# First batch's autoregressive taps as three single-pass products of two-term operands, and second terms loaded first at the joint of two attentions

## The chip, the cores and the metric

The kernel runs on one core of one Trainium2 chip. The metric is the device time of one execution in microseconds (us). A profiled execution gives the time of every instruction; its span is the time from the first to the last instruction in the profile.

## The reference, cut to what matters

An image batch of 2 x 128 channels x 64 x 64 passes through two layers. Layer 0 normalises in groups, forms queries, keys and values, adds rotary positions, attends over the 4096 positions in 4 heads, projects and adds. Layer 1 works on tokens t (2 x 4096 x 128):

```python
t = t + _L1_attn_ref(_ln_t(t))        # softmax(x x^T) x, unscaled, one head
t = t + _L1_ffn_ref(_ln_t(t), ...)    # spectral filters + autoregressive taps

def _compute_ar_u(Mu, u):             # Mu: (3, 128, 128)
    out = jnp.zeros(u.shape[:2] + (Mu.shape[-1],), dtype=u.dtype)
    for i in range(Mu.shape[0]):
        ui = jnp.pad(u, ((0, 0), (i, 0), (0, 0)))[:, :sl]
        out = out + jnp.einsum('btd,de->bte', ui, Mu[i])
    return out
```

The last step also convolves u with 16 spectral filters of full length, mixes the 16 results with 128 x 128 matrices, and does all of this on four prefixes of the sequence (whole, half, quarter, eighth), of which a softmax with a fixed Gumbel noise picks one (y_hard - y_soft + y_soft as weights). So one branch's taps `mu`, matrices and prefix length count; the kernel finds them at run time. All is float32.

## The kernel before, in words

One core does both batches in one instruction stream per engine. TensorE (PE) multiplies, VectorE (DVE), ScalarE (ACT) and GpSimd (POOL) work beside it, SyncE (SP) issues most DMAs. Waits between engines are placed by the framework. Within an engine it may also choose the order by readiness; instructions given to `keep_in_program_order` (layer 0's products L190, the layer norm's `normed` L716, the conv stage's matmuls through `ordered` L1133) stay in the order in which the code issues them. The generators passed as `beside` are advanced one step at a time between the pieces of the main work, so the code interleaves them by hand.

**Layer 0** (`layer0`, L175). For each batch, pair of heads and block of 512 positions it makes scores (L190), exponentials (L443), and weighted sums (L190 too), whose rows `close` (L386) copies to `accs` (L391). `divide` (L335) then adds the three value terms (L346, L348), takes reciprocals of the row sums by way of DRAM (L345, L349, L351, L352) and multiplies; `project` (L358) applies the output matrix. The last unit's `divide` (wait = 5) and `project` are not done when the attention ends; they go on as the generator `left` beside the next stage.

**Products of two terms.** Many operands are float32r pairs: a first term (a copy rounded to float32r) and a second term (the difference). A product is then three passes: first x first, first x second, second x first. `hiT`/`loT` hold the normalised tokens transposed, `hi`/`lo` untransposed. The second terms of batch 0 do not fit beside layer 0, so `normalise(0)` (L752) stores them in DRAM (`lows`, 8 chunks of two 128 x 512 tiles) and `ready(i)` (L1087) loads them back: for i = 0 the chunks 0 and 1, then chunk i + 1; each load goes into a tile `low` (one buffer, 512 KB), and two copies (L1092 to `loT`, L1093 to `lo`) follow.

**Attention of layer 1** (`attend`, L897), once per batch, over pairs of blocks (j, i), i from j to 7, of 512 tokens. `scores` (L906): three products a tile (L911), exponential on ACT (L920). `turn` (L924): transposes (L927), copy (L929), subtraction (L930). `sums` (L964): splits e into two terms (L968 on DVE or ACT, L969 on DVE), multiplies (`weigh`, L937), adds to `oT` (L975, L977). `close` (L945): the block's division and addition to the tokens (L948, L956, L959), then `closed(j)`.

- `attend(0)` runs beside `left`, batch 1's statistics, `filters` (L803), `matrices` (L857, with `branch_weights` L822: z at L830 and a chain of small DVE operations to wbr, coef at L872) and `normalise(1)` (L719, L766, L770). The transform table `fw` (L796) is loaded before it.
- `attend(1)` runs beside `feed(0)` (L1007): layer norm, transforms, and taps of batch 0. After each block, `closed(j)` (L1114) also loads two of the 16 mixing matrices (`m`, L1119, two buffers) and splits them.

**The taps** (`taps`, L1015; tiles of 512 tokens). `uT` holds 6 columns of 128 x 128: tokens transposed (L1051) and masked (L1052), and before them the last two columns of the tile before (L1054). Three float32 products per tile, of one matrix of `mu` each and four neighbouring columns of `uT` (L1024), are summed in PSUM, added to the tokens (L1027) and stored (`base`). Tile 0 needs the end of tile 7, so its taps come last (L1069 to L1077).

**The conv stage** (`convolve` L1176, `mix` L1203, `back` L1232) follows for both batches, its PE order written out; `feed(1)` runs beside it, with the same code for the taps.

Of the kernel before, what the change touches and what calls it, by code (L numbers as in the profile page):

```python
# [22 lines left out]
P = 128  # L23
# [12 lines left out]
NU = 3  # L36
# [27 lines left out]
def conv_attn_hybrid(ctx: ExitStack, tc: tile.TileContext, io):  # L64
# [110 lines left out]
    def layer0(tok, px, last, side, beside_last):  # L175
# [3 lines left out]
        with ExitStack() as l0:  # L179
# [155 lines left out]
            def divide(b, h, c, accs, wait):  # L335

                u = f"{b}_{h}_{c}"
                if h == 0:  # L340
                    ao[b, c] = (last if c == 3 else p1).tile([P, 1024], F32, tag=f"ao{c}", name=f"ao{b}_{c}", bufs=1)
                own = ao[b, c][CH * h : CH * h + CH, :]
                parts = [accs[CH * n : CH * n + CH, :] for n in range(NV)]
                rec = last.tile([CH, 1024 // CH], F32, tag="rec", name=f"rec{u}")
                nc.sync.dma_start(rec, accs[NV * CH :, :].rearrange("o (r s) -> o r s", r=CH))  # L345
                nc.vector.tensor_tensor(own, parts[0], parts[1], ALU.add)  # L346
                yield
                nc.vector.tensor_tensor(own, own, parts[2], ALU.add)  # L348
                nc.vector.reciprocal(rec, rec)  # L349
                back = dram.tile([CH, 1024 // CH], F32, tag="rec", name=f"back{u}", bufs=4)  # L350
                nc.sync.dma_start(back, rec)  # L351
                nc.sync.dma_start(parts[0], back.rearrange("r s -> (r s)").partition_broadcast(CH))  # L352
                for _ in range(wait):
                    yield
                nc.vector.tensor_tensor(own, own, parts[0], ALU.mult)
                yield
# [377 lines left out]
    def layers(st, layer0):  # L734
# [87 lines left out]
        def branch_weights(p):  # L822
# [4 lines left out]
            nc.gpsimd.dma_start(lg[:, 0, :], io["log_weights"].partition_broadcast(P))  # L827
            nc.gpsimd.dma_start(lg[:, 1, :], io["gumbel"].partition_broadcast(P))
            z = p.tile([P, NBR], F32, name="z")
            nc.vector.tensor_tensor(z, lg[:, 0, :], lg[:, 1, :], ALU.add)  # L830
            zm = p.tile([P, 1], F32, name="zm")
            nc.vector.tensor_reduce(zm, z, AX.X, ALU.max, negate=True)
            zs = p.tile([P, 1], F32, name="zs")
# [170 lines left out]
            for _ in beside:  # L1004
                pass

        def feed(b, p, bank, fw, stats=None):  # L1007


            if stats is None:  # L1010
                stats = LayerStats(p, tok[b], f"f{b}")
                yield from stats.steps()
            to = rows[b].rearrange("c r w d -> w c r d")

            def taps(i, uT):  # L1015
                oc = p.tile([P, 4, P], F32, tag="oc", name=f"oc{b}_{i}", bufs=1)
                pt = bank(f"tT{b}_{i}").rearrange("p (t c) -> p t c", c=C)
                for t in range(4):
                    nc.tensor.transpose(pt[:, t, :], tok[b][:, 4 * i + t, :], ident)
                nc.scalar.copy(oc, pt)  # L1020
                yield
                pa = bank(f"ar{b}_{i}").rearrange("p (t c) -> p t c", c=C)
                for n in range(NU):
                    nc.tensor.matmul(pa, mu[:, n, :], uT[:, 2 - n : 6 - n, :], start=(n == 0), stop=(n == NU - 1))  # L1024
                    if n == 0:
                        yield
                nc.vector.tensor_tensor(oc, pa, oc, ALU.add)  # L1027
                nc.sync.dma_start(base[b][:, 4 * i : 4 * i + 4, :], oc)
                yield

            before = first = None
            for i in range(NQ):
# [12 lines left out]
                    nc.sync.dma_start(to[:, c, at : at + 2, :], uhr[:, :, 1, :])  # L1045
                    yield

                uT = p.tile([P, 6, P], F32, tag="uT0" if i == 0 else "uT", name=f"uT{b}_{i}", bufs=1 if i == 0 else 2)
                pt = bank(f"uT{b}_{i}").rearrange("p (t c) -> p t c", c=C)
                for t in range(4):  # L1050
                    nc.tensor.transpose(pt[:, t, :], un[:, t, :], ident)  # L1051
                nc.vector.tensor_tensor(uT[:, 2:, :], pt, mask.unsqueeze(1).to_broadcast([P, 4, P]), ALU.mult)  # L1052
                if i:
                    nc.vector.tensor_copy(uT[:, :2, :], before[:, 4:, :])  # L1054
                    yield
                    yield from taps(i, uT)
                else:
# [4 lines left out]
            for c in range(2):  # L1062
# [3 lines left out]
            nc.sync.dma_start(to[:, :, BP, :], ul)  # L1066
            yield

            nc.gpsimd.memset(first[:, :2, 0:1], 0.0)  # L1069
            nc.vector.tensor_tensor(  # L1070
                first[:, :2, 1:],
                before[:, 4:, : P - 1],
                mask[:, 1:].unsqueeze(1).to_broadcast([P, 2, P - 1]),
                ALU.mult,
            )
            yield
            yield from taps(0, first)  # L1077

        with ExitStack() as l1:
            p1 = pool(l1, "l1")  # L1080
            lo.append(p1.tile([P, L], F32R, name="lo"))
            fw = transform(p1)
            with ExitStack() as part:
                p = pool(part, "l1_a")
                gate = [0]

                def ready(i):  # L1087
                    for n in range(2) if i == 0 else [i + 1]:
                        if n < NQ:
                            low = p.tile([P, 2, 512], F32, tag="low", name=f"low{n}")  # L1090
                            nc.sync.dma_start(low, lows[n].rearrange("n p c -> p n c"))
                            nc.vector.tensor_copy(loT[0][:, bass.ts(n, 512)], low[:, 0])  # L1092
                            nc.vector.tensor_copy(lo[0][:, bass.ts(n, 512)], low[:, 1])  # L1093

                def closed(j):
                    gate[0] = j + 1
# [13 lines left out]
            with ExitStack() as part:  # L1110
# [3 lines left out]
                def closed(j):  # L1114
                    fed.take(range(4 * j, 4 * j + 4))
                    fed.close(range(4 * j, 4 * j + 4))
                    own = slice(2 * j, 2 * j + 2)
                    m = p.tile([P, 2, 2, C], F32, tag="m", name=f"m{j}")
                    nc.sync.dma_start(m, mx[own].rearrange("k p s c -> p k s c"))  # L1119
                    nc.vector.tensor_copy(mxr[:, own], m)  # L1120
                    nc.vector.tensor_tensor(mxl[:, own], m, mxr[:, own], ALU.subtract)

                attend(1, p1, feed(0, p, bank, fw), closed)
        psum_a.close()


# [325 lines left out]
```

## Time and profile before

| what | value |
|---|---|
| median of 3 runs | 2924.3 us (2923.44 to 2927.81) |
| profiled execution | 2924.81 us |
| its span | 2923.0 us |
| mean granted clock of TensorE | 0.993 of full speed |
| chain that ended last | the conv stage: m L1218, bk L1272, vt L1262 on PE |
| layer 0's exponentials, L443 on ACT | 937.4 us in 704 instructions |
| layer 0's scores and sums, L190 on PE | 557.7 and 557.1 us |
| conv stage's mixing, L1218 on PE (three groups) | 409.5, 403.0, 291.8 us |
| loads tables_in<-tables on SP | 1024 of 64 KB, 3.3 us from issue to landing |

The profiled execution's time is 1.8 us more than its span. A group of the profile names the line, engine, operation, the tile written and the tiles read, then count, busy time and mean length; a matmul's length includes its latency, so neighbouring matmuls overlap, and the spacing of their starts tells what one costs. A float32 matmul leaves two records. The waits of an engine name the line that waited, the engine and line that released it, and the time. The layer-0 attention ends and the first attention of layer 1 begins near 1028 us; the second attention begins near 1396 us and ends before 1770 us.

### The profile page before, as it was taken

The page shows a single profiled execution, that of the slowest core. Times are in us where ns is not written, and L with a number is a line of the kernel's source. Part 1 is how long each engine was busy: PE and PEld are TensorE (multiplying, and loading weights), DVE is VectorE, ACT ScalarE, POOL GpSimd, SP SyncE. Part 2 cuts the span into 40 slices and gives each one's busy share as a digit, 9 for nine tenths or more (in the row PEclk, how much of TensorE's full clock was granted, in tenths as well). Part 3 has the DMA queues.
Part 4 walks back from the last instruction along what each step waited for, and adds up shares of the span by engine and source line. Part 5 has one row for each costly group of instructions (what it writes and reads, how often), then busy time and mean ns, then how long its engine had stood idle before and what let it go on. Part 6 is the DMA issues. An engine that isn't in the chain of part 4 may idle for free. (4 is left out here: it accounts for less than half of the span.)

```text
span 2923.0 us, 40062 instructions
## 1 busy us (share of the span) xinstructions
PE 2852.4 (98%) x13872; PEld 1815.1 (62%) x13872; DVE 1689.9 (58%) x2916; ACT 1916.1 (66%) x2507; POOL 653.8 (22%) x1312
## 2 busy tenths in 40 slices
PE   5999999999999999999999999999999999999998
PEld 3555555555455577787777885666666666666665
DVE  5265562355243289877866677555555555555554
ACT  4999999999999956565555664444444444444442
POOL 3022120022000010000102003343444444444440
PEclk9999999999999999999999999999999999999999
DMA  4122120021001024100011002333333334333331
GB/s 137 33 63 77 48 66 16 5 78 48 6 33 35 4 83 128 57 1 1 26 39 40 8 26 68 97 89 93 92 85 82 81 77 115 82 85 84 82 82 54
DMA packets 166033, 175.91 MB, mean 60 GB/s; under 512 B 45264, under 2 KB 109536, under 8 KB 165824
## 3 DMA queue, kind: packets, MB, share of 16 engines
q1 hardware_dynamic: 122528, 137.05, 16.9%
q0 software_dynamic: 40304, 32.99, 5.4%
q10 hardware_dynamic: 2992, 3.22, 0.3%
q8 instruction: 115, 1.88, 0.3%
q14 instruction: 94, 0.77, 0.1%
HBM read 130.68 MB, written 25.49 MB: 53 GB/s over the span
## 5 line engine op out<-in xcount | busy, mean ns | idle before, releaser
L443 ACT ACTIVATE e<-s 128x1536 f16<-128x1536 f32 (+1 forms) x704 | 937.4, 1427 | 34.8 <-PE s L190 29.6
L1196 DVE TENSOR_TENSOR xl<-cv,xh 128x1024 fp32r<-128x1024 f32 x512 | 603.2, 1220 | 436.3 <-ACT xh L1195 349.0
L1195 ACT CAST xh<-cv 128x1024 fp32r<-128x1024 f32 x512 | 494.6, 1018 | 522.7 <-PE cv L1186 511.8
L1161 POOL DMA_DIRECT2D tokens_in<-rows x1024 | 490.5, 487 | 680.0 <-PE cv L1186 580.7
L190 PE MATMUL s<-qs,ks 128*128 128x512 f16 x2048 | 557.7, 379 | 11.8 <-ACT e L443 7.4
L190 PE MATMUL acc<-e,v 128*97 128x512 f16 x2048 | 557.1, 379 | 3.3 <-DVE accs L391 0.2
L1218 PE MATMUL m<-xh,loT 128*128 128x512 f32 x1024 | 409.5, 400 | 0.0
L1218 PE MATMUL m<-xh,hiT 128*128 128x512 f32 x1024 | 403.0, 394 | 0.0
L190 PEld LDWEIGHTS <-v 128*97 128x97 bf16 x2048 | 254.5, 124 | 214.3 <-issue 11.8
L190 PEld LDWEIGHTS <-ks 128*128 128x128 f16 x2048 | 200.5, 99 | 232.6 <-issue 46.9
L920 ACT ACTIVATE ey<-y,nshift 128x512 f32<-128x512 f32 x288 | 195.9, 689 | 201.4 <-PE y L911 179.2
L1186 PE MATMUL cv<-tables_in,tokens_in 32*128 32x512 f32 x2048 | 300.3, 646 | 1.8 <-DVE xl L1196 1.8
L1218 PE MATMUL m<-xl,hiT 128*128 128x512 f32 x1024 | 291.8, 417 | 1.2 <-DVE xl L1196 0.5
L1218 PEld LDWEIGHTS m<-xl,hiT 128*128 128x128 f32 x1024 | 178.6, 189 | 175.7 <-issue 104.7
L1218 PEld LDWEIGHTS m<-xh,loT 128*128 128x128 f32 x1024 | 192.5, 188 | 90.7 <-issue 47.8
L1218 PEld LDWEIGHTS m<-xh,hiT 128*128 128x128 f32 x1024 | 192.3, 188 | 42.2
L930 DVE TENSOR_TENSOR eT<-eT,eT 128x512 fp32r<-128x512 f32 x224 | 147.3, 684 | 112.9 <-ACT eT L929 112.0
L937 PE MATMUL oacc<-ep,hi 128*128 128x512 f32 x576 | 209.1, 411 | 1.2 <-DVE ep L969 1.2
L969 DVE TENSOR_TENSOR ep<-ey,ep 128x512 fp32r<-128x512 f32 x288 | 191.3, 684 | 7.6 <-PE oacc L937 1.4
L391 DVE COPY accs<-acc 97x512 f32<-97x512 f32 x64 | 44.2, 691 | 253.3 <-PE acc L190 253.3
L929 ACT ACTIVATE eT<-eT 128x512 fp32r<-128x512 f32 x224 | 133.1, 605 | 55.7 <-PE eT L927 55.5
L937 PE MATMUL oacc<-eT,hi 128*128 128x512 f32 x448 | 154.1, 405 | 2.2 <-DVE oT L975 1.2
(197 smaller groups left out, 3031.3 us busy)
## 6 DMA issues: line engine op xcount, KB each, us to landing
tables_in<-tables SPq DMA_DIRECT2D x1024, 64.0 KB, 3.3
tab<-in_rot SPq DMA_DIRECT2D x32, 512.0 KB, 4.1
tokens_in<-rows POOLq DMA_DIRECT2D x1024, 16.0 KB, 3.2
rows<-uh SPq DMA_DIRECT2D x64, 128.0 KB, 1.9
qs<-term POOLq DMA_DIRECT2D x112, 64.0 KB, 2.0
ks<-term POOLq DMA_DIRECT2D x96, 64.0 KB, 1.9
accs<-back SPq DMA_DIRECT2D x32, 128.0 KB, 2.3
lows<-stage SPq DMA_DIRECT2D x16, 256.0 KB, 2.0
```

The costliest lines, as they stand in the source:

```text
L190: tc.keep_in_program_order(nc.tensor.matmul(*args, **kw))
L443: nc.scalar.activation(e[:, own, :], ps[:, own, :], AF.Exp, scale=SCORE_SCALE)
L920: nc.scalar.activation(e[:, 2 * h + q, :], ps[:, q, :], AF.Exp, bias=nshift, accum_out=den[:, t, i : i + 1])
L929: nc.scalar.activation(eT[0], pt, AF.Copy, accum_out=den[:, 4 * i + u, j : j + 1])
L930: nc.vector.tensor_tensor(eT[1], pt, eT[0], ALU.subtract)
L937: nc.tensor.matmul(acc, a[0][:, own], c, start=(start and t == 0 and n == 0), stop=(stop and t == len(es) - 1 and n == 2),)
L969: nc.vector.tensor_tensor(es[t][1], e[:, t, :], es[t][0], ALU.subtract)
L1161: nc.gpsimd.dma_start(ut[part, :, :], rows[b][ci, row : row + BP, w0 : w0 + WC // 2, :])
L1186: nc.tensor.matmul(pu[:, h, :], ut[grp, w % 2, :], tt[grp, w % 2, :], start=True, stop=True)
L1195: nc.scalar.copy(hi, pu.rearrange("d h (c k) -> d k h c", k=NK))
L1196: nc.vector.tensor_tensor(seconds[n % 2][:, :, w, 64 * g2 : 64 * g2 + 64].rearrange("d k (h c) -> d k h c", h=2), pu.rearrange("d h (c k) ...
L1218: nc.tensor.matmul(acc, m, x, start=(s == 0 and w == 0 and i == 0), stop=(s == 1 and w == WC - 1 and i == len(products) - 1),)
```

## The change

`feed` takes a new argument `parts`, set for the first batch alone. With it, `mu` and the masked `uT` are each split into two float32r terms by a copy and a subtraction (`split`), the columns that are taken over from the tile before are copied for both terms, and each tap is three products instead of one float32 product; the masked columns go through a tile that shares the buffer of `oc`, and tiles 1 to 7 share one buffer a term for `uT`. `ready(i)` becomes `second_parts`: chunk 0 is issued ahead of the load of `fw`, and `ready(i)` issues chunk i + 1 alone. Its first copy, the sum z in `branch_weights`, and the first sum of the last `divide` are kept in program order. The tile `m` has one buffer instead of two.

```diff
@@ -343,7 +343,9 @@
                 parts = [accs[CH * n : CH * n + CH, :] for n in range(NV)]
                 rec = last.tile([CH, 1024 // CH], F32, tag="rec", name=f"rec{u}")
                 nc.sync.dma_start(rec, accs[NV * CH :, :].rearrange("o (r s) -> o r s", r=CH))
-                nc.vector.tensor_tensor(own, parts[0], parts[1], ALU.add)
+                terms = nc.vector.tensor_tensor(own, parts[0], parts[1], ALU.add)
+                if wait > 1:
+                    tc.keep_in_program_order(terms)
                 yield
                 nc.vector.tensor_tensor(own, own, parts[2], ALU.add)
                 nc.vector.reciprocal(rec, rec)
@@ -827,7 +829,7 @@
             nc.gpsimd.dma_start(lg[:, 0, :], io["log_weights"].partition_broadcast(P))
             nc.gpsimd.dma_start(lg[:, 1, :], io["gumbel"].partition_broadcast(P))
             z = p.tile([P, NBR], F32, name="z")
-            nc.vector.tensor_tensor(z, lg[:, 0, :], lg[:, 1, :], ALU.add)
+            tc.keep_in_program_order(nc.vector.tensor_tensor(z, lg[:, 0, :], lg[:, 1, :], ALU.add))
             zm = p.tile([P, 1], F32, name="zm")
             nc.vector.tensor_reduce(zm, z, AX.X, ALU.max, negate=True)
             zs = p.tile([P, 1], F32, name="zs")
@@ -1004,13 +1006,23 @@
             for _ in beside:
                 pass

-        def feed(b, p, bank, fw, stats=None):
+        def feed(b, p, bank, fw, stats=None, parts=False):


             if stats is None:
                 stats = LayerStats(p, tok[b], f"f{b}")
                 yield from stats.steps()
             to = rows[b].rearrange("c r w d -> w c r d")
+
+            def split(x, out):
+                nc.vector.tensor_copy(out[0], x)
+                nc.vector.tensor_tensor(out[1], x, out[0], ALU.subtract)
+
+            mus, passes = [mu], [(0, 0)]
+            if parts:
+                mus = [p.tile([P, NU, C], F32R, name=f"mu_{n}", bufs=1) for n in range(2)]
+                split(mu, mus)
+                passes = [(0, 0), (1, 0), (0, 1)]

             def taps(i, uT):
                 oc = p.tile([P, 4, P], F32, tag="oc", name=f"oc{b}_{i}", bufs=1)
@@ -1021,7 +1033,14 @@
                 yield
                 pa = bank(f"ar{b}_{i}").rearrange("p (t c) -> p t c", c=C)
                 for n in range(NU):
-                    nc.tensor.matmul(pa, mu[:, n, :], uT[:, 2 - n : 6 - n, :], start=(n == 0), stop=(n == NU - 1))
+                    for m, u in passes:
+                        nc.tensor.matmul(
+                            pa,
+                            mus[m][:, n, :],
+                            uT[u][:, 2 - n : 6 - n, :],
+                            start=(n == 0 and (m, u) == passes[0]),
+                            stop=(n == NU - 1 and (m, u) == passes[-1]),
+                        )
                     if n == 0:
                         yield
                 nc.vector.tensor_tensor(oc, pa, oc, ALU.add)
@@ -1045,13 +1064,29 @@
                     nc.sync.dma_start(to[:, c, at : at + 2, :], uhr[:, :, 1, :])
                     yield

-                uT = p.tile([P, 6, P], F32, tag="uT0" if i == 0 else "uT", name=f"uT{b}_{i}", bufs=1 if i == 0 else 2)
+
+                if i < 2 or not parts:
+                    uT = [
+                        p.tile(
+                            [P, 6, P],
+                            F32R if parts else F32,
+                            tag=f"uT0_{n}" if i == 0 else f"uT_{n}",
+                            name=f"uT{n}_{b}_{i}",
+                            bufs=1 if i == 0 or parts else 2,
+                        )
+                        for n in range(2 if parts else 1)
+                    ]
                 pt = bank(f"uT{b}_{i}").rearrange("p (t c) -> p t c", c=C)
                 for t in range(4):
                     nc.tensor.transpose(pt[:, t, :], un[:, t, :], ident)
-                nc.vector.tensor_tensor(uT[:, 2:, :], pt, mask.unsqueeze(1).to_broadcast([P, 4, P]), ALU.mult)
+                masked = p.tile([P, 4, P], F32, tag="oc", name=f"masked{i}", bufs=1) if parts else uT[0][:, 2:, :]
+                nc.vector.tensor_tensor(masked, pt, mask.unsqueeze(1).to_broadcast([P, 4, P]), ALU.mult)
                 if i:
-                    nc.vector.tensor_copy(uT[:, :2, :], before[:, 4:, :])
+                    for x, y in zip(uT, before):
+                        nc.vector.tensor_copy(x[:, :2, :], y[:, 4:, :])
+                if parts:
+                    split(masked, [x[:, 2:, :] for x in uT])
+                if i:
                     yield
                     yield from taps(i, uT)
                 else:
@@ -1066,31 +1101,38 @@
             nc.sync.dma_start(to[:, :, BP, :], ul)
             yield

-            nc.gpsimd.memset(first[:, :2, 0:1], 0.0)
-            nc.vector.tensor_tensor(
-                first[:, :2, 1:],
-                before[:, 4:, : P - 1],
-                mask[:, 1:].unsqueeze(1).to_broadcast([P, 2, P - 1]),
-                ALU.mult,
-            )
+            for x, y in zip(first, before):
+                nc.gpsimd.memset(x[:, :2, 0:1].bitcast(F32) if parts else x[:, :2, 0:1], 0.0)
+                nc.vector.tensor_tensor(
+                    x[:, :2, 1:],
+                    y[:, 4:, : P - 1],
+                    mask[:, 1:].unsqueeze(1).to_broadcast([P, 2, P - 1]),
+                    ALU.mult,
+                )
             yield
             yield from taps(0, first)

         with ExitStack() as l1:
             p1 = pool(l1, "l1")
             lo.append(p1.tile([P, L], F32R, name="lo"))
-            fw = transform(p1)
             with ExitStack() as part:
                 p = pool(part, "l1_a")
                 gate = [0]

+                def second_parts(n):
+                    if n < NQ:
+                        low = p.tile([P, 2, 512], F32, tag="low", name=f"low{n}")
+                        nc.sync.dma_start(low, lows[n].rearrange("n p c -> p n c"))
+                        copy = nc.vector.tensor_copy(loT[0][:, bass.ts(n, 512)], low[:, 0])
+                        if n == 0:
+                            tc.keep_in_program_order(copy)
+                        nc.vector.tensor_copy(lo[0][:, bass.ts(n, 512)], low[:, 1])
+
                 def ready(i):
-                    for n in range(2) if i == 0 else [i + 1]:
-                        if n < NQ:
-                            low = p.tile([P, 2, 512], F32, tag="low", name=f"low{n}")
-                            nc.sync.dma_start(low, lows[n].rearrange("n p c -> p n c"))
-                            nc.vector.tensor_copy(loT[0][:, bass.ts(n, 512)], low[:, 0])
-                            nc.vector.tensor_copy(lo[0][:, bass.ts(n, 512)], low[:, 1])
+                    second_parts(i + 1)
+
+                second_parts(0)
+                fw = transform(p1)

                 def closed(j):
                     gate[0] = j + 1
@@ -1115,12 +1157,12 @@
                     fed.take(range(4 * j, 4 * j + 4))
                     fed.close(range(4 * j, 4 * j + 4))
                     own = slice(2 * j, 2 * j + 2)
-                    m = p.tile([P, 2, 2, C], F32, tag="m", name=f"m{j}")
+                    m = p.tile([P, 2, 2, C], F32, tag="m", name=f"m{j}", bufs=1)
                     nc.sync.dma_start(m, mx[own].rearrange("k p s c -> p k s c"))
                     nc.vector.tensor_copy(mxr[:, own], m)
                     nc.vector.tensor_tensor(mxl[:, own], m, mxr[:, own], ALU.subtract)

-                attend(1, p1, feed(0, p, bank, fw), closed)
+                attend(1, p1, feed(0, p, bank, fw, parts=True), closed)
         psum_a.close()


```

## The prediction

> **What bounds the kernel now.** I read four views in this order: the page's totals, the waits of PE, the timeline around the joint, and the busy time by stretch.
>
> ```profile
> PE 2852.4 (98%) x13872; PEld 1815.1 (62%) x13872; DVE 1689.9 (58%) x2916; ACT 1916.1 (66%) x2507; POOL 653.8 (22%) x1312
> ```
>
> TensorE (PE) is busy for 2852.4 of 2923.0 us. So a saving counts when it shortens PE's work or one of its few gaps. The waits of PE between 1023 and 1400 us (line waited for, total, times, longest) show the gap at the joint, where layer 0's attention hands over to the first attention of layer 1:
>
> ```profile
> PE y L911 <- DVE loT L1092: 5.1, 1, 5.1
> PE eT L927 <- DVE loT L770: 1.7, 1, 1.7
> PE yT L766 <- DVE y L719: 1.6, 1, 1.6
> ```
>
> The timeline (start, length) shows how it comes about:
>
> ```profile
> 1025.47 0.35 SPq L796 DMA_DIRECT2D fw<-in_fw  x1
> 1025.88 0.42 SPq L1091 DMA_DIRECT2D low<-lows  x1
> ...
> 1027.16 0.81 PE L911 MATMUL y<-hiT 128*128 128x512 f32 x2
> 1027.55 0.69 DVE L391 COPY accs<-acc 97x512 f32<-97x512 f32 x1 [4.67 <-PE acc L190]
> ...
> 1028.30 1.22 DVE L346 TENSOR_TENSOR ao<-accs 32x1024 f32<-32x1024 f32 x1
> 1029.55 1.22 DVE L348 TENSOR_TENSOR ao<-ao,accs 32x1024 f32<-32x1024 f32 x1
> ...
> 1032.57 0.42 DVE L1092 CAST loT<-low 128x512 fp32r<-128x512 f32 x1
> 1033.04 0.79 PE L911 MATMUL y<-loT,hiT 128*128 128x512 f32 x1 [5.06 <-DVE loT L1092]
> ...
> 1033.63 0.63 PE L911 MATMUL y<-hiT,loT 128*128 128x512 f32 x1
> 1034.06 0.63 PE L911 MATMUL y<-hiT 128*128 128x512 f32 x1
> ```
>
> PE has two of the three products of the first scores, then waits for the second term loT. Its load was issued at 1025.88, behind fw's on SP's queue, and its copy stands on VectorE (DVE) behind two sums of `divide` (L346, L348) and the start of the branch weights. When PE resumes, single passes start 0.43 us apart instead of the usual 0.23, until about 1036.6. By stretch (length; PE, PEld, DVE, ACT, POOL busy with counts; PE clock; DMA share; GB/s):
>
> ```profile
> 1028.24:1200.00 171.76, 163.66 (x808) 130.65 (x808) 159.97 (x425) 98.26 (x276) 12.17 (x13) 0.98 0.35 108
> 1180.00:1200.00 20.00, 17.97 (x89) 13.55 (x87) 19.60 (x54) 8.48 (x24) 0.10 (x1) 1.00 0.38 112
> 1396.00:1580.00 184.00, 181.83 (x838) 131.25 (x837) 125.74 (x309) 100.74 (x270) 18.50 (x25) 1.00 0.12 37
> 1400.00:1420.00 20.00, 18.35 (x83) 12.99 (x82) 19.83 (x83) 11.85 (x33) 8.69 (x7) 1.00 0.05 14
> ```
>
> After the joint DVE is nearly full (93%, and 98% just before 1200), and PE falls short of 20 us there. In the second attention, with the taps, DVE is at 68% and PE at 99%, except for the first 20 us.
>
> [...]
>
> **The change, part by part.** The groups that price it (busy, mean ns, idle before), then two taps in PE's timeline:
>
> ```profile
> L1024 PE MATMUL ar<-uT,mu 128*128 128x512 f32 x96 | 46.6, 594 | 0.0
> L1054 DVE COPY uT<-uT 128x256 f32<-128x256 f32 x14 | 4.1, 291 | 0.3
> L968 DVE CAST ep<-ey 128x512 fp32r<-128x512 f32 x144 | 59.4, 418 | 17.4 <-PE oacc L937 16.1 <-ACT ey L920 0.8
> L969 DVE TENSOR_TENSOR ep<-ey,ep 128x512 fp32r<-128x512 f32 x288 | 191.3, 684 | 7.6 <-PE oacc L937 1.4 <-ACT ep L968 1.3
> 1440.82 1.88 PE L1024 MATMUL ar<-uT,mu 128*128 128x512 f32 x4
> 1442.54 0.60 PE L927 MATMUL eT<-ident,ey 128*128 128x128 f32 x4
> ```
>
> *1. Taps on PE.* The first batch has 8 tiles of 3 taps, 24 float32 products; each leaves two records, so 48 of the 96 are its own. The mean of 594 ns is latency, since neighbours overlap: two taps (four records) start at 1440.82 and the next work at 1442.54, so a tap takes 1.72/2 = 0.86 us. Afterwards it is three single passes on float32r operands, as y and oacc are made of now, whose starts lie 0.23 us apart (0.69). From 24 x 0.86 = 20.6 to 72 x 0.23 = 16.6 us: -4.1 us, nearly all on the path, since PE has 2.2 us idle in those 184. Bounds of a pass: 0.22 to 0.24 us, the neighbouring spacings, so -4.8 to -3.4.
>
> *2. Splitting on DVE.* Each of 8 tiles gets a copy (0.42, L968's row) and a subtraction (0.68, L969's): 8.8 us. The history copy L1054 is doubled: 7 x 0.29 = 2.0. The first tile's masked copy: 0.4. The split of mu (128x384): three quarters of 0.42 and 0.68, 0.8 to 0.9. Sum 12.1 us. All but the last hide in the 58 us that DVE has idle in 1396 to 1580; its share goes from 68% to about 75%. mu's split falls where DVE is full (1400 to 1420): +0.9 charged whole; bounds 0 and 2. Without cover the rest would cost up to 11.2. The single uT buffer makes the history copy wait for PE's taps of the tile before, but the sum L1027 queued next to it on DVE waits for the same taps; `masked` takes oc's buffer and waits for oc's store, which was issued long before. Both taken as nothing; up to 0.3 a tile (2 us) if the order is unlucky. None is a gain, as neither takes work away. GpSimd's doubled memset is off the path for the same reason.
>
> *3. The joint.* The first second-term load now stands on SP ahead of fw, and waits only for old transfers of GpSimd's queue, no longer for PE: it lands tens of us early. Its copy comes on DVE directly after accs (ends 1028.24) and a memset of 0.06. Copy at about 1028.3 to 1028.7; from copy to product was 1033.04 - 32.57 = 0.47 us, so PE resumes at about 1028.75, 4.3 us earlier. The idle is 0.8 us[...]: 9 products no longer pay the extra 0.20 us, 1.8 us more. But PE can't keep all of it: the second chunk's load (3.4 us or more from issue to landing, its single buffer freed only by the first chunk's two copies) and ScalarE's exponentials come next. Walking the rows through, I find the second chunk's first loT product 5.3 us earlier than its 1039.08. Behind DVE's reordered queue: the two sums (2.44 us) and the branch-weight chain (about 2.4 us of DVE and ACT round trip before L1092, and as much after) are not removed; they now follow, kept in order, some after the filter tables. What waits for them is off PE's path: ao's projection, coef and mask. The loads of fw, phi, gw and rec on SP follow the moved one; none is waited for at the joint by PE.
>
> That backlog of some 4.9 us meets a DVE that is 93% busy until 1200, where PE already waits for it (L770, L719, 3.3 us). DVE's 160.0 us of work leave 11.8 idle between 1028.24 and 1200. Afterwards 2.4 us idle are left near the joint, and 3 to 6.5 later where DVE waits for others; so its end moves from 11.8 to between 5.4 and 8.9 us of idle time: a gain of 2.9 to 6.4. I take -4.5; outer bounds -7 (PE's whole gap and clock, nothing paid back) and 0 (all paid back).
>
> *4. m in one buffer.* m7's load must now wait for m6's subtraction and lands about 2.9 us after it, at about 1763.0, when its cast is due near 1762.6 and PE waits 1.2 us for DVE's oT (L975). +0.3; bounds 0 and 2. The other m loads have tens of us. The conv stage's order is written out and unchanged: 0.
>
> **Sum.** -4.1 + 0.9 - 4.5 + 0.3 = -7.4 us. The span of 2923.0 becomes 2915.6; with the 1.8 us outside it (2924.81 - 2923.0), 2917.4. The profiled run lies 0.5 above the median of 2924.3, so against the median: **2916.9 us**.
>
> **Rivals.** *A, nothing paid back at the joint.* -4.1 + 0.9 - 7 + 0.3 = -9.9, 2914.4; with mu's split hidden too, 2913.5. For it: DVE has idle time before 1140. Against: PE waits for DVE at 1190. *B, the joint's gain is paid back whole* where DVE is full: -4.1 + 0.9 + 0 + 0.3 = -2.9, 2921.4. For it: DVE at 98% in 1180 to 1200. Against: DVE itself idled for 4.67 us and more around the joint. *C, the second term still comes late*, with the load or copy moved only on paper: the same 2921.4, but with PE's wait of 5 us in place. The instruction orders speak against it. *D, slower: VectorE sets the pace* in both attentions. Then PE's savings in taps and joint count nothing, and DVE's 12.1 us of new work count one for one: 2924.3 + 12.1 + 0.3 = 2936.7. It decides from where DVE's share nears 98%, as in 1180 to 1200; for it, the stretch 1400 to 1420; against, the 75% of the rest.
>
> **How the numbers follow.** My forecast 0.52, A 0.17, B 0.20, C 0.04, D 0.07. The forecast's own range is 2914.5 to 2919.5 (joint -6.4 to -2.9, a pass 0.22 to 0.24), a fifth of it above the mark of 2918.45. A measurement of this kernel can tell about 0.2%, 5.85 us, from no change: faster below 2918.45, slower above 2930.15. Faster 0.42 + 0.17 = 0.59; same 0.10 + 0.20 + 0.04 = 0.34; slower 0.07. The range reaches from A with a better pass, 2912, to B with 1.6 us of unlucky waits from parts 2 and 4, 2923; D and the tails beyond are the 2 in 10 left out.
>
> **What would show it.** Step 1: 48 records of float32 taps left and 72 new ones 0.23 us apart. Step 2: DVE about 12 us busier in the second attention, with no new wait of PE for ep, eT or oc; a row of such waits of over 4 us means D. Step 3: PE's wait for loT at the joint under 1 us and the clock near 1.00; then waits at L719 and L770 as long as now mean my value, 4 us longer mean B, shorter ones A. Step 4: PE's wait for oT near 1765 grows by less than 1 us. I am wrong if the loT wait remains, or if the second attention's length changes by other than about -3.2 us.

## The result, and the profile after

| | before | after |
|---|---|---|
| median of 20 runs each | 2924.76 us | 2920.64 us |
| lowest to highest | 2922.84 to 2927.81 | 2918.05 to 2923.39 |
| profiled execution | 2924.81 us | 2921.34 us |
| its span | 2923.0 us | 2919.5 us |

The ratio is 0.9986, with a 95% interval of 0.9980 to 0.9992. So the change makes the kernel faster, by 4.1 us, less than the 0.2% set as the mark. The forecast was -7.4 us; rival B (the joint's gain paid back) had 2921.4. The page's first row after:

```profile
PE 2849.5 (98%) x13896; PEld 1819.0 (62%) x13896; DVE 1697.7 (58%) x2942; ACT 1916.3 (66%) x2507; POOL 652.6 (22%) x1313
```

**Where the time went.** Layer 0's attention issues the same work in both, and yet the last copy of accs comes 0.51 us later in the profiled execution of after; over all executions shown below this varies from 1.5 us earlier to 0.5 us later. So I count from that copy. The table gives the start of the k-th of the 288 exponentials of layer 1's two attentions against before, and in the last column that of the conv stage's first copy, xh; both come from the starts in the traces. "ey0" is the joint, "ey64" the end of the full stretch, "ey152" to "ey160" VectorE's full stretch in the second attention, "ey160" to "ey216" the taps.

```
                  ey0    ey32   ey48   ey64   ey72   ey152  ey156  ey160  ey216  ey280   xh0
before (us)     1035.6 1109.1 1146.6 1187.1 1210.9  1400.7 1409.0 1420.5 1598.6 1752.2 1775.3
after            -5.48  -3.45  -3.36  +0.44  -0.63   -0.68  +1.07  +1.16  -3.63  -3.86  -4.20
joint alone      -5.47  -4.16  -3.87  -0.56  -2.28   -2.28  -2.28  -2.29  -2.32  -2.54  -2.56
taps alone       -0.20  -0.19  +0.25  +0.23  -0.24   -0.27  +1.47  +3.14  -1.62  -1.78  -2.12
mu written later -5.47  -3.32  -3.26  +0.44  -0.86   -0.85  +1.03  +6.23  -0.86  -1.10  -1.44
mu kept later    -5.47  -4.24  -3.99  -0.79  -3.56   -3.48  -3.49  -3.48  -7.93  -8.08  -8.42
rec kept         -5.47  -3.43  -3.05  +0.79  -0.39   -0.11  +1.64  +3.29  -1.43  -1.63  -1.95
weights, 1st     +1.39  +1.08  +1.69  +2.16  +1.95   +1.95  +3.68  +5.16  +0.41  +0.24  -0.10
weights, 2nd     -5.49  -3.10  -3.47  -0.52  -1.89   -3.23  -1.50  -1.41  -6.19  -6.46  -6.79
copies on ACT    -5.47  -3.10  -3.98  -3.13  -4.54   -5.95  -4.21  -4.11  -8.58  -8.81  -9.16
light before     +0.07  +0.32  +1.96  +5.65  -1.34   -1.70  -1.71  -1.70  -1.65  -1.84  -1.82
light after      -5.48  -3.90  -0.63  -0.76  -7.86   -8.17  -6.41  -6.31 -11.00 -11.17 -11.52
all three        -5.49  -1.19  -2.66  -1.57  -2.79   -4.13  -4.14  -4.13  -8.58  -8.78  -9.13
```

The row of after says it in four figures: 5.5 us ahead at the joint, 0.7 left at the second attention, 1.75 lost there at once (ey152 to ey156), 4.7 won from there to the end of the taps. All rows are single executions. Where two kernels issue their instructions in different orders, a column inside a stretch also shows which work came first: light before is 5.65 us late at ey64 and 1.34 early at ey72. So the columns behind the stretch, ey72 and ey152, are the ones to compare.

*The clock.* The traces also record when TensorE's clock was granted at half. Between 1000 and 1700 us it was so for these stretches (start and length, us):

```
before            1030.2 6.83   1200.9 3.41
after             1034.3 3.41   1201.6 3.41
joint alone       1200.0 3.41
taps alone        1029.2 6.83   1199.9 3.41   1411.5 3.41
mu written later  1034.1 3.41   1201.3 3.41   1409.5 6.83
mu kept later     none
rec kept          1198.8 6.83   1410.4 3.41
weights, 1st      1031.3 6.83   1202.0 6.83   1413.6 3.41
weights, 2nd      1188.4 3.41
copies on ACT     none
light before      1030.3 6.83
light after       none
all three         1035.5 3.41
```

These stretches explain part of the differences between the rows, as the experiments show.

*The joint.* The first second term is now copied as soon as accs is (start, length, engine and line):

```profile
1028.06 0.69 DVE L393 COPY accs<-acc 97x512 f32<-97x512 f32 x1 [4.67 <-PE acc L190]
1028.68 0.42 DVE L1126 CAST loT<-low 128x512 fp32r<-128x512 f32 x1
...
1029.15 0.50 PE L913 MATMUL y<-loT,hiT 128*128 128x512 f32 x1 [0.67 <-DVE loT L1126]
...
1032.83 0.34 DVE L351 RECIPROCAL rec<-rec 32x32 f32<-32x32 f32 x1 [3.38 <-DMA rec<-accs]
1033.10 0.35 DVE L970 CAST ep<-ey 128x512 fp32r<-128x512 f32 x1
```

PE waits 0.67 us instead of 5.06. The waits of PE between 1023 and 1400 us, which had loT at 5.1 us on top:

```profile
PE oacc L939 <- DVE ep L970: 2.7, 2, 1.8
PE eT L929 <- DVE loT L772: 1.7, 1, 1.7
...
PE y L913 <- DVE loT L1126: 1.1, 2, 0.7
...
PE yT L768 <- DVE y L721: 0.6, 1, 0.6
```

A new wait, for ep, stands on top. It is the next thing late: the reciprocal of the row sums now stands ahead of the first split of e, and VectorE idles 3.38 us for its transfer. VectorE's waits between 1027 and 1212 us (line waited for, total, times, longest) hold two that the kernel before did not have, at rec and, of this size, at zs:

```profile
DVE eT L932 <- ACT eT L931: 4.7, 11, 1.2
...
DVE rec L351 <- DMA rec<-accs: 3.4, 1, 3.4
DVE zs L838 <- ACT soft L837: 2.0, 1, 2.0
DVE pm L728 <- DMA raw<-in_mpm: 1.6, 3, 0.8
DVE loT L1126 <- DMA low<-lows: 1.6, 2, 1.2
```

And PE, by stretch (columns as before):

```profile
1028.75:1200.00 171.25, 164.90 (x808) 129.76 (x808) 158.23 (x425) 98.00 (x276) 12.42 (x13) 0.99 0.35 107
...
1180.00:1200.00 20.00, 16.64 (x75) 11.41 (x73) 19.24 (x52) 5.50 (x15) 0.10 (x1) 1.00 0.39 117
1400.00:1420.00 20.00, 17.30 (x76) 11.81 (x74) 19.85 (x83) 11.38 (x31) 7.05 (x7) 1.00 0.05 14
1396.00:1580.00 184.00, 180.81 (x872) 136.88 (x871) 137.07 (x341) 101.58 (x272) 17.27 (x25) 1.00 0.12 37
```

In 1180 to 1200 PE is busy 16.64 us where it was 17.97: it does less there although it arrived early. From 1400 to 1420 it has 17.30 against 18.35.

*The taps.* Three and six passes where there were two and four records:

```profile
1440.65 0.97 PE L1037 MATMUL ar<-uT,mu 128*128 128x512 f32 x3
1441.46 0.60 PE L929 MATMUL eT<-ident,ey 128*128 128x128 f32 x4
1441.82 1.64 PE L1037 MATMUL ar<-uT,mu 128*128 128x512 f32 x6
1443.29 0.40 PE L939 MATMUL oacc<-ep,hi 128*128 128x512 f32 x1
```

### The profile page after: what moved, and what is told of

It is laid out like the page before. It is cut to its first block, busy times and chain, and to the rows that moved or that the text cites. A ratio compares the mean times of both kernels' runs of the same rounds, so it can differ in the third digit from the quotient of the medians.

```text
span 2919.5 us, 40111 instructions
## 1 busy us (share of the span) xinstructions
PE 2849.5 (98%) x13896; PEld 1819.0 (62%) x13896; DVE 1697.7 (58%) x2942; ACT 1916.3 (66%) x2507; POOL 652.6 (22%) x1313
## 3 DMA queue, kind: packets, MB, share of 16 engines
q8 instruction: 115, 1.88, 0.3%
## 5 line engine op out<-in xcount | busy, mean ns | idle before, releaser
L190 PE MATMUL s<-qs,ks 128*128 128x512 f16 x2048 | 557.7, 379 | 11.8 <-ACT e L445 7.4
L190 PEld LDWEIGHTS <-v 128*97 128x97 bf16 x2048 | 254.6, 124 | 214.3 <-issue 11.8
```

Of the source, the lines that this page charges most:

```text
L190: tc.keep_in_program_order(nc.tensor.matmul(*args, **kw))
```

## The experiments

Theory T: from the joint to 1200 us VectorE sets the pace. Between the accs copy and the second loT subtraction of batch 1, its work fell only from 160.7 to 158.9 us, and its idle time rose from 11.8 to 13.0, so the head start at the joint is given back but for 0.6 us. Rival R1: the joint keeps its gain, and the second attention loses. Rival R2: that stretch has another pace-maker (PE, or the loads of the matrices). Medians are compared with the kernel before in the same runs.

**The joint alone, and the taps alone.**

```diff
-                attend(1, p1, feed(0, p, bank, fw, parts=True), closed)
+                attend(1, p1, feed(0, p, bank, fw), closed)
```

That is the first, with m's two buffers put back. The second keeps `parts=True` and has the old joint, with no order kept:

```diff
+            fw = transform(p1)
...
-                    second_parts(i + 1)
-                second_parts(0)
-                fw = transform(p1)
+                    for n in range(2) if i == 0 else [i + 1]:
+                        ...
```

> The joint alone: second terms loaded first and the three orders kept, but float32 taps in the second attention and two buffers for m, as before. Theory T (VectorE paces the stretch from the joint to 1200 us; the new order makes it wait 3.4 us for rec's transfer and 2.0 us for zs, so its idle time does not shrink and the head start at the joint is given back): about 0.6 us faster than before, 2924.1. Rival R1 (the joint keeps its 4.5 us and something in the second attention lost them): about 2920.3.

> The taps alone: single-pass taps of two-term operands for the first batch, m in one buffer, but the joint as before (fw loaded first, no order kept). Theory T: the second attention's gain is whole, -4.8 for the taps and +1.85 for splitting mu and -0.5 beyond, so 3.5 us faster than before, 2921.2. Rival R1: it gains little, within 1 us of 2924.8. By stretch T expects the exponentials of the second attention to run 3 us ahead of before by 1600 us, after falling 1.8 us behind by 1420.

Measured: joint 2922.71 against 2925.13 (0.9991, 0.9983 to 0.9999), -2.4 us; taps 2922.25 (0.9990, 0.9984 to 0.9997), -2.9 us. -2.4 and -2.9 add to more than the -4.1 of the whole, but the intervals are wider than that difference. The joint alone falls between the two expectations. From the accs copy to the second attention it issues the same work as the whole change, in the same order on every engine, and so do the kernels "mu written later" and "mu kept later"; yet at ey152 after, the joint alone and these two stand at -0.68, -2.28, -0.85 and -3.48. So the joint's net gain is no fixed number: it scatters over 3 us. The clock goes with it: it stood at half for two stretches of 3.41 us in after and in mu written later, for one in the joint alone, and for none in mu kept later, which puts each such stretch at 1.2 to 1.4 us (an estimate from these four figures). (The landing of the matrices' loads differs too: VectorE's waits for raw near 1163 and 1190 are 0.67 and 0.76 us in after; in the joint alone, one of 0.18 and none.) The clock is not all: mu kept later, without half clock, lost 1.9 of its 5.5 us by ey72, while the kernel before, against which this is counted, ran at half clock for 3.41 us from 1200.9; so about 3 us (an estimate, 1.9 + 1.3) were taken back by something else. The first half of R1 falls: these four lost 1.9 to 4.9 us of the head start by ey72. The taps alone show +1.74 between ey152 and ey156 and -4.8 from ey160 on, as in the whole.

**mu's split moved.** Written after the first tile's columns, and then also kept there:

```diff
                 else:
                     first = uT
                     yield
+                    if parts:
+                        split(mu, mus, tc.keep_in_program_order)
```

In the first run `split(mu, mus)` stands there without the last argument.

> The whole change, but mu is split after the first tile's columns, past the layer-norm statistics where VectorE is 99% busy. If the split (0.87 us of VectorE work in line with PE's operands) causes the 1.85 us lost between 1400 and 1420, that loss goes to about 0 and the kernel is 1.8 us faster than the changed one, 2918.8. Rival (the loss there is the scheduler's order of the statistics, or waits that follow anyway): 2920.6, with the 1.85 us still lost.

> The whole change, with both operations of mu's split kept in program order after the first tile's columns; in the run with the split only written later, the scheduler had put its copy back among the statistics. If the split's place costs the 1.7 us lost between 1400 and 1420 (and the half clock that some runs then show near 1411), both go: no loss by 1420, 1.7 to 3.4 us faster than the changed kernel, 2917.2 to 2918.9. Rival (another part of the taps' work reorders that stretch): still 1.7 us behind at 1420, 2920.6.

Measured: written later 2921.15 against 2925.13 (0.9987, 0.9980 to 0.9994), no different from the change. Only the split's subtraction had moved, to 1421.5; its copy still stands among the statistics (in after at 1403.11), and 1.88 us are lost there:

```profile
1402.71 0.33 DVE L1018 CAST mu<-mu 128x384 fp32r<-128x384 f32 x1
```

Kept: 2917.07 against 2924.04 (0.9976, 0.9967 to 0.9986), -7.0 us, and the row of the table is flat from ey152 to ey160. Every row with the split's copy in this stretch loses 1.73 to 1.88 us from ey152 to ey156, and the rows without it (joint alone, light before, mu kept later, all three) nothing. So the split's place is the cause: 0.87 us of VectorE work (0.34 + 0.53) where VectorE is 99% busy cost 1.75 us, twice its length. VectorE's order tells where the rest comes from. From ey152 to its next copy to oT, for whose end PE waits 0.8 us, it takes 8.90 us in before and in mu kept later, and 10.62 in after. From start to start, 0.68 us of the 1.72 are the split; 1.04 are nine more operations of the statistics (four at L702, four at L705, one at L88), which in the new order come ahead of that copy. Of the 2.9 us by which this median beats the change's, the split's place accounts for 1.75; the rest is open (its profiled execution was already 2.8 us ahead of after at ey152, before the moved code, with no half clock).

More hangs on the split's place. The windows of 5 us near 1411 for the taps alone, then for mu kept later:

```profile
1410.00:1415.00 5.00, 4.22 (x12) 3.17 (x12) 5.00 (x25) 4.17 (x12) 3.02 (x3) 0.66 0.00 0
```

```profile
1410.00:1415.00 5.00, 5.00 (x26) 3.75 (x25) 4.90 (x15) 2.24 (x6) 3.38 (x2) 1.00 0.13 36
```

With the split in the full stretch, PE's clock (third column from the end, 0.66 and 1.00 here) sometimes falls to half there: in the profiled executions of taps alone, mu written later, rec kept and weights, 1st, and not in those of after, weights, 2nd, copies on ACT and light after. Where it falls, 1.9 to 3.3 us are won from ey156 to ey216, and 4.4 to 4.7 where it does not.

**rec's reciprocal kept in order.**

```diff
-                nc.vector.reciprocal(rec, rec)
+                turned = nc.vector.reciprocal(rec, rec)
+                if wait > 1:
+                    tc.keep_in_program_order(turned)
```

> The whole change, but the reciprocal of the last unit's row sums is also kept in program order, so that VectorE no longer stands still 3.4 us for rec's transfer ahead of the first splits of e. Theory T (VectorE paces to 1200): PE's 1.76 us wait and half clock near 1034 go, and VectorE's idle time to 1200 shrinks by 2 to 3.4 us: 2917.2 to 2918.6. Rival R2 (the loads of the matrices, or PE, pace that stretch, so VectorE only idles elsewhere): 2920.6, the head start again given back by 1200.

Measured: 2921.17 against 2925.13 (0.9986, 0.9979 to 0.9992), -4.0 us, as the whole change. The 3.38 us wait is gone, and two others stand in its place:

```profile
1029.43 0.43 DVE L972 CAST ep<-ey 128x512 fp32r<-128x512 f32 x1 [1.98 <-ACT ey L924]
...
1033.26 0.43 DVE L1128 CAST loT<-low 128x512 fp32r<-128x512 f32 x1 [2.07 <-DMA low<-lows]
```

VectorE's idle time to the same point is 13.2 us, not less. The half clock near 1034 went, as expected, but one of 6.83 us came at 1198.8. So the wait at rec is not the cause by itself; behind it VectorE waits for the exponentials and for the second chunk's load, and this part of T was wrong.

**Branch weights in layer 0.** The chain from z to wbr is called from `beside_last`; `matrices` takes its result. The second version also keeps rec and coef in order.

```diff
+            picked.append(branch_weights(last))
             yield from normalise(0, stats, lambda i, n: stages[n][:, i])
...
-            wbr = branch_weights(p)
+            wbr, top = picked[0]
```

> The whole change, but the branch weights (z to wbr, a chain of about 3 us of VectorE and ScalarE work with a 2.0 us wait for zs in it) are computed during layer 0's last attention, where VectorE has idle time. Theory T (VectorE paces the stretch from the joint to 1200): the stretch shortens by the wait and the work that left it, 4 to 5 us, so 2915.6 to 2916.6. Rival R2 (something else paces it): 2920.6.

> The whole change, with the branch weights computed in layer 0, rec's reciprocal kept in order, and coef kept in order too; in the run with branch weights in layer 0 alone, coef had moved ahead of loT and VectorE stood 4.8 us waiting for sig. Theory T (VectorE's work and waits to 1200 set the stretch): the 2.0 us wait for zs and some 3 us of the chain are gone, so 2 to 5 us faster than the changed kernel, 2915.6 to 2918.6. Rival R2 (something else paces it): 2920.6.

Measured: the first, 2923.51 against 2925.40 (0.9992, 0.9984 to 1.0000), loses what the joint gains. With wbr ready, coef was put ahead of the second term, and it waits for GpSimd's sig:

```profile
1033.09 1.01 DVE L875 TENSOR_SCALAR coef<-wbr,sig 128x4 f32<-128x4 f32 x7 [4.79 <-POOL sig L872]
1034.02 0.42 DVE L1127 CAST loT<-low 128x512 fp32r<-128x512 f32 x1
```

The second: 2917.11 against 2924.04 (0.9976, 0.9967 to 0.9985), -6.9 us, 2.8 better than the change, in the range of T. Its profile does not tell how: the idle time to the same point is 13.4 us, and it is 1.3 us ahead of after at ey72 and 2.5 at ey152, no more than single executions scatter. How the gain comes about is open.

**VectorE lightened.** First by leaving out two of the four terms of the matrices' sums, in the kernel before and in the changed one; then, with nothing left out, by moving copies to ScalarE:

```diff
-        for i in range(1, NBR):
+        for i in range(1, terms):
...
-                weighted_sum(pm, raw, coef[:, k, :])
+                weighted_sum(pm, raw, coef[:, k, :], 2)
```

```diff
-                    (nc.scalar.copy if t % 2 else nc.vector.tensor_copy)(es[t][0], e[:, t, :])
+                    (nc.scalar.copy if t % 2 or (b == 0 and j < 2) else nc.vector.tensor_copy)(es[t][0], e[:, t, :])
```

> The kernel before, with only two of the four terms of the matrices' weighted sum (the other two are left out: 32 VectorE operations of 0.47 us, 15 us, between 1110 and 1200 us). Theory T: VectorE no longer paces the end of that stretch; PE does, and gets back part of the 8 us that it lacks there: 3 to 6 us faster, 2919 to 2922. Rival R2 (loads or PE pace it): no change, 2924.8.

> The changed kernel with the same two terms of the matrices' sum left out. Theory T: with VectorE no longer full, the head start at the joint is kept, so this is 7 to 9 us faster than the kernel before with the same omission: 2911 to 2914. Rival R2 (the head start is lost whatever VectorE's load): 4.2 us faster than the lightened kernel before, as the two full kernels differ.

> The whole change, with all four first-term copies of e on ScalarE, instead of two, in the first two block rows of the first attention: about 30 copies of 0.42 us, 12 us, leave VectorE between 1036 and 1200, and 30 of 0.61, 18 us, come to ScalarE, which is busy 57% there. Nothing is left out. Theory T (VectorE paces that stretch): the joint's head start is kept, 5 to 7 us faster than the changed kernel, 2913.6 to 2915.6. Rival R2 (its pace comes from elsewhere) or ScalarE's copies late for PE: 2920.6 or slower.

Measured: light before 2921.41 against 2925.40 (0.9986, 0.9979 to 0.9992); light after 2913.34 (0.9958, 0.9944 to 0.9971). Between the two lie 8.1 us, where the two full kernels lie 4.1 apart: beside a lighter VectorE the same change is worth twice as much. At ey152 the joint is worth 8.17 - 1.70 = 6.5 us, in the four full executions 0.7 to 3.5. PE in the last 60 us of the stretch, for the changed kernel and for light after:

```profile
1140.00:1200.00 60.00, 56.20 (x274) 43.41 (x272) 57.66 (x144) 30.52 (x85) 0.10 (x1) 1.00 0.42 125
```

```profile
1140.00:1200.00 60.00, 58.64 (x299) 47.61 (x298) 53.98 (x124) 34.36 (x98) 0.10 (x1) 1.00 0.38 114
```

VectorE 57.66 against 53.98 us, PE 56.20 against 58.64: with less work on VectorE, PE stands still less. This is what T expects. But the pair does not shut out R2. With two terms left out, VectorE waits for the matrices' loads, longer in light before than in light after (waits between 1028 and 1200 us; 1.9 and 1.6 us in the full kernels):

```profile
DVE pm L726 <- DMA raw<-in_mpm: 8.4, 8, 2.2
```

```profile
DVE pm L728 <- DMA raw<-in_mpm: 4.1, 7, 1.1
```

In the 60 us above, PE is busy for only 55.81 us in light before, less than the 57.47 of the full kernel before, though VectorE has 51.54 us of work there. The clock differs as well: it was at half twice in after and never in light after. And the order of PE's products changes with each of these edits. So how much of the doubled gain is VectorE's room, and how much the loads, the clock and the order, is not shown.

The copies on ScalarE give 2918.18 against 2924.04 (0.9982, 0.9973 to 0.9990), -5.9 us: 1.7 us better than the change, less than the 5 to 7 expected. (Its profiled execution, without half clock, is the fastest of its runs, so its row in the table shows more.)

**All together.** First rec kept, the first version of branch weights and mu written later; then rec, the second version, mu kept later and the copies on ScalarE.

> The three edits together on top of the change: rec's reciprocal kept in order, branch weights computed in layer 0, mu split late. Theory T: -2.7 - 4.5 - 1.8 = -9 against the changed kernel, less 1 to 2 where PE becomes the bound: 2911.6 to 2913.6. Rival R2: only mu's 1.8, 2918.8.

> The three edits that each helped, together on top of the change: mu's split kept behind the statistics (2.9 us better than the changed kernel against the kernel before of its runs), branch weights in layer 0 with rec's reciprocal and coef kept in order (2.8), first-term copies of e on ScalarE in the first two block rows of the first attention (1.7). Theory T (VectorE's work and waits set both full stretches): mu's adds whole, the other two act on the same stretch and add only until PE is the bound there (it lacked 8 us in all): 6.5 to 7.5 us faster than the changed kernel, 11 us faster than before, 2913.0. Rival (the first attention's stretch has another bound that either edit alone already reaches): 9 to 10 us faster than before, 2914 to 2915.

Measured: the first 2925.22 against 2925.40 (0.9998, 0.9990 to 1.0006): it inherits coef ahead of loT. The second 2915.35 against 2925.76 (0.9965, 0.9951 to 0.9978), -10.4 us, the fastest kernel that leaves nothing out. It lies between the rival's expectation (9 to 10) and T's (11), and the interval holds both. VectorE now idles 20.8 us between the accs copy and the end of the stretch; 4.5 us of that are six waits of 0.4 to 1.5 us for the matrices' loads, in front of pm, and 5.0 one wait for the second chunk. So once VectorE has room it waits for the loads that R2 spoke of; that they then set the pace is not shown. VectorE's waits between 1028 and 1200 us:

```profile
DVE loT L1131 <- DMA low<-lows: 5.9, 2, 5.0
...
DVE pm L730 <- DMA raw<-in_mpm: 4.5, 6, 1.5
```

## Why the prediction was right and wrong

The time lies in the stated range and the sign is right; the size is little more than half, and the likeliest case was not the one that came. (With the terms stated for it, the forecast's own range is 2914.3 to 2919.2, not 2914.5 to 2919.5.)

1. *Taps, -4.1 expected, -4.7 measured in after from ey156 to ey216, -4.8 in taps alone and -4.4 in mu kept later from ey160.* The mechanism is right and the size inside its bounds (-4.8 to -3.4). Where the gain stands is not where the prediction put it. Summing from each matmul's start to the next between ey160 and ey216, for the kernel before and for mu kept later, which has the same number of y, eT and uT rows: the ar rows take 17.4 and 17.6 us, no gain; y falls from 44.4 to 41.9 and oacc from 80.1 to 78.7. The product behind a float32 tap starts early and lasts longer (at 1459.06 in before, 0.05 us after the tap's second record for 0.23, and 0.77 us for 0.39), so part of a tap's cost stands in its successor's row: the ten y and oacc products right behind taps take 3.6 us more than ten others. With these the float32 taps cost 17.4 + 3.6 = 21.0 us, about the 20.6 expected. The new passes cost 17.6/72 = 0.244 us, not 0.23. So the taps themselves give 3.4 us, the least that the bounds allow; most of the last 1.0 us stands in the three kinds of transposes (25.8 to 25.0), and why is open.

2. *Splitting on VectorE, +0.9 expected, +1.75 measured.* The 11.2 us of tile splits were hidden as said: VectorE goes from 125.7 to 137.1 us of 184, and from 1421 to 1600 us PE waits for no other engine. The single uT buffer makes the history copy wait 7.0 us in two places, and nobody waits for that. mu's split was the mis-sized term, inside the bounds of 0 and 2: I charged its length and took the order around it as given, and nine operations of the statistics moved ahead with it. The errors of 1 and 2 offset each other: from ey152 to ey216 after wins 2.95 us where -4.1 + 0.9 = -3.2 was forecast, and that this agrees so well is in part luck.

3. *The joint, -4.5 expected, -0.7 in the profiled execution and -2.4 alone.* The step that failed is "Afterwards 2.4 us idle are left near the joint, and 3 to 6.5 later": 13.0 us were left, not 5.4 to 8.9. PE's resumption came as worked out (0.67 us of idle for 0.8). But I took VectorE's waits to vanish with PE's, and did not ask where, in the new order, an instruction with a pending transfer would stand at the head of VectorE's queue: rec (3.38 us), the second chunk (1.22) and zs (2.04). The second chunk's load, reckoned at 3.4 us or more, took 5.7 from its issue at 1030.02, so the chunk's first loT product came at 1036.21, 2.9 us earlier than before and not 5.3. The 1.8 us that I counted for the clock rested on its staying at full speed after 0.8 us of idle, which the trace of before did not show. After the wait of 0.67 us it did stay, but after the next one, of 1.76 us for ep, it was at half from 1034.3 to 1037.7, and again from 1201.6. The sign given for it failed too: the waits at L719 and L770 (now L721 and L772) fell from 3.3 to 2.3 us, which was to mean rival A; PE waited elsewhere, for ep. Of the rivals B came nearest. Its reason, deferred work, does not fit: VectorE's work in the stretch fell by 1.8 us, and its waits moved and grew. That VectorE's fullness takes back part of the gain is supported by the light pair, but not separated from the loads and the clock; which of the waits matters most is not settled, since removing one alone brought up the next.

4. *m in one buffer, +0.3 expected, no loss measured.* From ey216 to the conv stage after gains 0.57, the joint alone, with two buffers, 0.24; PE's wait for oT is 0.9 us where it was 1.2.

## What to carry to other kernels

A gap closed on the engine that bounds the kernel can be lost again to the engine that runs full next to it (5.5 us at the joint were 0.7 at the second attention here): make the ledger of that second engine's idle time, line by line in the new order, and ask for each instruction at the head of its queue which transfer or engine it would wait for (rec here, 3.38 us). Work put among operations of a full engine can cost twice its length (0.87 us of work on a VectorE that was 99% busy cost 1.75), when other work comes ahead with it; here moving it by a few steps won that back. Before explaining 1 or 2 us by such a ledger, compare when the clock was at half: four executions with the same instruction order lay 2.8 us apart. An order that a scheduler chooses has to be looked up again after every edit: twice here an instruction that had become free moved ahead of the one that mattered.

## What the runs showed of the hardware that I had not expected

PE's clock was at half in 19 stretches of the table above, 12 of 3.41 us and 7 of 6.83 us. Some came behind a long wait, some behind short ones. In before PE waited 5.06 us at the joint, and the clock fell at 1030.2, within that wait. In after it fell at 1034.3, behind a wait of 1.76 us that ended at 1033.5. In mu written later it fell at 1409.5, where the longest of PE's waits since 1405 was 1.05 us, and in the taps alone at 1411.5, where it was 0.93. Yet the clock of after stayed at full speed beside the same work there, with nearly the same waits (until, length, us):

```
                  ep           ep           ep           oT           clock falls at
taps alone    1406.91 0.35  1408.57 0.93  1409.69 0.15  1410.97 0.78  1411.5
after         1407.81 0.35  1409.46 0.92  1410.59 0.15  1411.86 0.78  -
```

In the 3.42 us before the fall PE was busy for 2.00 us in the taps alone. In after it was busy for 1.99 us from 1408.97 to 1412.39, the same stretch of its work. (These busy times are estimates, as the ends of matmuls are modelled.) What decides whether the clock falls at such a point is not shown. Up to the second attention, four executions with the same order of instructions had two, one, two and no stretch at half, and lay 2.8 us apart.

Behind a float32 matmul of two records, a single-pass matmul has a longer record: in nine of ten such cases in the second attention of before it is 0.77 to 0.8 us long instead of 0.39, and the matmul after it starts 0.61 to 0.64 us later instead of 0.23.
